# A graph attention layer: two of each batch's row gathers become 256 loads of one row each, from SP and ACT

## The chip, the cores and the metric

The kernel runs on one core of a Trainium2 chip. A core has five engines that run side by side: PE (TensorE, matrix products), DVE (VectorE), ACT (ScalarE), POOL (GpSimd) and SP (SyncE, which here only issues DMAs). Each works through its own instructions in order and waits for others by semaphores. DMAs are carried out by 16 DMA engines; they are issued by SP and ACT (hardware queues) and by POOL (a software queue). The metric is the time of one execution on the device in microseconds (us), as a median of several runs.

## The reference, cut to what matters

There are 12,500 nodes with 128 features and 412,500 edges, sorted by their target node; every edge has 64 features of its own. The layer normalizes the nodes, projects them, scores each edge from its two ends and its features, takes a softmax over the edges of each target, and adds the weighted sum of the source rows.

```
h = relu(layernorm(x)) @ W_node.T            # 4 heads of 32
e = edge_attr @ W_edge.T
att = leaky_relu(sum(concat[h[src], h[tgt], e] * a))
ex = exp(att - max over the edges of tgt)
w = ex / (sum of ex over the edges of tgt + (edges - degree) * exp(-m))
out = x + sum over the edges of tgt of w * h[src]
```

## The kernel before, in words

**Prologue** (lines 191 to 487). The nodes are normalized and projected once, and the results are written to a table in DRAM with one row of 144 floats (576 bytes, ROW) per node: for each head 32 values, two columns of ones, and the source's part of the score; at the end the target's part of the score for the four heads. Constants such as `least_b` (the byte address in the table of the lowest target of each chunk) and `pens` (where a segment begins) are made here too.

**Main loop** (lines 835 to 873). The edges are cut into chunks of 896 (7 tiles of 128, T = 7), 8 chunks make a batch (CB = 8), and there are 58 batches (NBT). A batch has 56 tiles; for each edge of a tile, one on each of the 128 partitions, the source's row is needed in `hs` (128 partitions x 56 tiles x 144 floats). There are two such buffers, one for the even and one for the odd batches. Tile 2 of each batch (FIRST) is not loaded from the table: its rows are projected anew by `normalize`, `project` and `keep_rows`. The other 55 are gathered by POOL in `gather` (line 547), one indirect DMA for each tile.

One turn `b` of the loop issues its work in this order, each engine taking its own part of it:

- SP: the indices of batch b+2 (line 187), then in `load` for batch b+1 the edge features `eft` (line 518), the targets `mem` (line 521), a register load of eight addresses (line 523), eight small loads `twb` from the table at register addresses (line 528), and `drawn` (line 533).
- POOL: `gather` for batch b+1. Ahead of its first gather stands a copy of `sums` into `gate` (line 550); `sums` is written by ACT at the end of the scatter of batch b-1 (line 684), the last user of the same `hs` buffer. So POOL begins only when that buffer is free.
- `weigh` of batch b (line 625): DVE waits until the rows have landed (`landed`, line 582; a wait on a semaphore that counts these loads), turns the scores (`zst`, line 629), then DVE and ACT in turn add them and make the leaky ReLU (lines 637 to 639, ACT's part L638), DVE makes two scans for the maximum of each segment (lines 641 and 643), ACT the exponentials (line 647), DVE the rest.
- SP: `pen` of batch b+1 (line 591), and the stores of finished outputs (line 820).
- `scatter` of batch b (line 655): DVE multiplies the rows by their weights (line 666); PE sums them with matrix products against `hot` (line 674) in three groups of chunks; ACT copies each group's results from PSUM to `r` (line 697), and `sums` in the last group (line 684).
- `normalize`, `begin` and `project` for batch b+1: ACT's L561, PE's products of edge features and targets (lines 602 and 606), DVE's masks (lines 597 to 621), among them `hot`, which waits until PE has used the old one.
- Every second batch `merge` (line 699), in which ACT makes two exponentials (lines 717 and 719) between two parts of DVE's work; then `keep_rows`; in about every fourth batch `finish` (line 784), where ACT makes an exponential (line 795) and 16 copies (line 810) that wait for DVE.

Everything is in this order because the loop stands under a manual schedule: no instruction is moved past another on its engine. Loads that go through `by_itself` (line 575) are counted by a semaphore of their own, and only `landed` waits for them.

Of the kernel before, what the change touches and what calls it, by code (L numbers as in the profile page):

```python
# [18 lines left out]
P = 128  # L19
# [11 lines left out]
SB = 4  # L31
# [26 lines left out]
LOGIT = EROW * 4  # L58
FIRST = 2
EPS = 1e-5  # L60


def tiles_of(sc):

    return [T if c < NCH - 1 else LAST for c in (2 * sc, 2 * sc + 1) if c < NCH]


# [37 lines left out]
def kernel(  # L105
# [4 lines left out]
    ahead: bass.AP,  # L110
    dstc: bass.AP,
    ef: bass.AP,
    w_node: bass.AP,
# [66 lines left out]
    row_sems = [tc.alloc_semaphore(f"rows{k}") for k in range(ROWSEMS)]  # L180
    row_done = [0] * ROWSEMS

    indices = ctx.enter_context(tc.tile_pool(name="indices", bufs=3))
# [7 lines left out]
    with (  # L191
# [7 lines left out]
        wn = p1.tile([P, D], F32, name="wn")  # L199
        nc.scalar.dma_start(wn, w_node)  # L200
        we = p1.tile([P, 2, K], F32, name="we")
        for s in range(2):
# [231 lines left out]
        for s in range(2):  # L434
            for j in range(SB):
                at = (2 * j + s) * H
                nc.vector.tensor_copy(wa3[s * K:(s + 1) * K, j, at:at + H], pe[s * K:(s + 1) * K, :])

        for g in range(NG):
            extent(g)  # L440
            load_extents(g + 2, min(g + 3, NG))
# [72 lines left out]
    def load(s):  # L514
# [17 lines left out]
        s.drawn = work.tile([P, D], F32, name="drawn")  # L532
        nc.sync.dma_start(s.drawn, drawn[:, s.b, :])
        s.hs = (work if s.b % 2 else even).tile([P, SB * CT, ROW], F32, name="hs")
        s.tiles = []
        for t in range(T):
            for sc in range(s.b * SB, (s.b + 1) * SB):
                held = tiles_of(sc) + [0, 0]
                for c in range(2):
                    i = (sc - s.b * SB) * CT + c * T + t  # L540
                    if t < held[c]:
                        if i != FIRST:
                            s.tiles.append(i)
                    else:
                        nc.vector.memset(s.hs[:, i, :], 0.0)
# [29 lines left out]
    def by_itself(load, group, sems, done, k):  # L575

        load.then_inc(sems[k], 16)
        done[k] += 16
        tc.add_to_no_dep_group(group, load.ins)
        tc.no_tile_sem_insts.add(load.ins.name)  # L580

    def landed(engine, group, sems, done, k, *what):
# [41 lines left out]

    def weigh(s):

        landed(nc.vector, f"rows{s.b}", row_sems, row_done, s.b % ROWSEMS, s.hs[:, :, :], s.ends[:, :, :, :])
        zst = work.tile([P, T, R], F32, name="zst")
# [4 lines left out]
        def grouped(what, g):  # L633
            return what.rearrange("r (t g i) -> r g t i", g=NQT, i=R)[:, g, :, :]

        for g in range(NQT):
            nc.vector.tensor_tensor(grouped(s.z, g), grouped(s.z, g), zst[g * R:(g + 1) * R, :, :], op=OP.add)  # L637
            nc.scalar.activation(grouped(att, g), grouped(s.z, g), AF.Identity, scale=0.2)  # L638
        nc.vector.tensor_tensor(s.z, s.z, att, op=OP.max)
        up = ps.tile([P, BANKS * 512], F32, name="up")[:R, :CE]  # L640
# [5 lines left out]
        for g in range(NQT):  # L646
            nc.scalar.activation(both[g * R:(g + 1) * R, 0, :, :], grouped(att, g), AF.Exp)  # L647
        for g in range(NQT):
            nc.vector.scalar_tensor_tensor(both[g * R:(g + 1) * R, 1, :, :], grouped(s.pen[:, 1:], g), -1.0 / BIG,  # L649
                                           grouped(m, g), op0=OP.mult, op1=OP.mult)  # L650
# [185 lines left out]
    with tc.manual_schedule():  # L836
        for b in range(-1, NBT):
            if b == -1:
                for k in range(2):
                    batch(k).ends = early[k]  # L840
                load_pen(batch(0))
            elif b + 2 < NBT:
                batch(b + 2).ends = index(b + 2)
            if b + 1 < NBT:
                load(batch(b + 1))
                gather(batch(b + 1), sums if b >= 1 else None)
            if b >= 0:
                s = batch(b)
                weigh(s)
                if b + 1 < NBT:  # L850
                    load_pen(batch(b + 1))
                for store in stores:
                    store()
                stores.clear()
                scatter(s)
            if b + 1 < NBT:
                normalize(batch(b + 1))
                begin(batch(b + 1))
                project(batch(b + 1))
            if b >= 0:  # L860
                first, last = merge_of(b)
                if b == last:
                    merge(first * CB, chunks_of(first, last))
                del batches[b]
            if b + 1 < NBT:
                keep_rows(batch(b + 1))
            if b == 3:
                count_windows()
            for b0, n, behind in parts():
                if behind == b:  # L870
                    stores.append(finish(work, ps, "up", em_ps, b0, n, b + 2 < NBT))
        for store in stores:
            store()
# [253 lines left out]
```

## Time and profile before

| | us |
|---|---|
| median of 3 runs | 4961.14 (4951.02 to 4962.55) |
| profiled execution | 4916.85 |
| its span | 4914.7 |
| busy: POOL | 3063.8 (62%) |
| busy: DVE | 1848.6 (38%) |
| busy: PE | 1798.9 (37%) |
| busy: ACT | 750.8 (15%) |

The profile is of one execution. Busy time counts work on data; instructions that load registers, wait, or issue DMAs from SP and ACT are not in it, so SP has no busy time at all though it issues hundreds of DMAs. Its instructions are seen in the timeline and in the view of one source line, with the letter q behind the engine's name. A line of the timeline gives start, duration, engine, line, operation, output<-input, the number of merged instructions, and in brackets the idle time before it with what ended it ("issue": nothing that the profile shows; "remote": an unknown releaser). A line of a group gives the count, the busy time in us and the mean of one in ns, then the idle time of the engine just before such instructions and what ended most of it.

### The profile page before, as it was taken

What the parts mean: (1) busy time and instruction counts of PE and PEld (TensorE: products, weight loads), DVE (VectorE), ACT (ScalarE), POOL (GpSimd) and SP (SyncE); (2) the same over time, 40 slices, a digit from 0 to 9 for tenths busy, and PEclk for the clock granted to TensorE, in tenths of its full rate; (3) what the DMA queues carried; (4) which work ended last, traced back from release to release, by engine and by line L of the source; (5) the groups of instructions that cost most, each with busy time, mean ns of one, the idle gap of its engine ahead of it and who ended that gap; (6) DMA issues with size and microseconds to landing.
All of it is one profiled execution on the core that took longest, in us unless ns stands there. A gap on an engine that the chain in (4) does not pass through costs nothing.

```text
span 4914.7 us, 22169 instructions
## 1 busy us (share of the span) xinstructions
PE 1798.9 (37%) x4479; PEld 719.8 (15%) x4479; DVE 1848.6 (38%) x3602; ACT 750.8 (15%) x2842; POOL 3063.8 (62%) x3295
## 2 busy tenths in 40 slices
PE   3133333343334333344334432433333333443243
PEld 2111111111111111111111111111111111111112
DVE  3424343424343343334342434334333433342335
ACT  3111111111111111111111111111111111111111
POOL 4446656666666666666666666666666666666661
PEclk7566666666666666667667665666666666666676
DMA  4333333333333333333332333333333333332431
GB/s 143 116 85 86 80 104 83 97 92 90 91 93 93 85 99 77 103 78 106 76 103 77 106 87 96 89 90 96 83 98 82 100 80 101 77 106 72 106 81 39
DMA packets 214923, 447.92 MB, mean 91 GB/s; under 512 B 86498, under 2 KB 119774, under 8 KB 214526
## 3 DMA queue, kind: packets, MB, share of 16 engines
q0 software_dynamic: 103136, 237.36, 21.1%
q1 hardware_dynamic: 108926, 201.71, 12.7%
q10 hardware_dynamic: 2720, 7.39, 0.4%
q14 instruction: 103, 0.84, 0.1%
q8 instruction: 38, 0.62, 0.1%
HBM read 427.11 MB, written 19.09 MB: 91 GB/s over the span
## 4 chain that ended last, share of the span: by engine, by line
another core or an unknown queue 33%; issue 25%; PE 16%; DVE 12%; ACT 11%; DVEq 1%; DMA 1%; ACTq 0%; SPq 0%
PE pa L674 8%; ACT r L697 7%; PE z L602 6%; PE z L606 2%; DVE up L641 2%; DVE m L643 1%; ACT both L647 1%; DVE z L637 1%; ACT a L638 1%; DVE acc L744 1%; ACT up L810 1%; DVE a L644 1%; DVE hs L666 1%; DVE a L735 1%
## 5 line engine op out<-in xcount | busy, mean ns | idle before, releaser
L552 POOL DMA_INDIRECT hs<-table,ends x3165 | 2997.2, 947 | 1072.4 <-issue 996.3
L674 PE MATMUL pa<-hs,hot 128*96 128x420 f32 (+2 forms) x2526 | 1037.1, 581 | 1872.7 <-issue 1244.7
L674 PEld LDWEIGHTS pa<-hs,hot 128*96 128x96 f32 (+2 forms) x2526 | 472.6, 192 | 2420.8 <-issue 2271.0
L697 ACT COPY r<-pa 32x35 f32<-32x35 f32 x1842 | 384.9, 209 | 2184.8 <-remote 1529.1
L621 DVE TENSOR_TENSOR hot<-exr,key 128x448 f32<-128x448 f32 x231 | 137.2, 621 | 1375.5 <-remote 1177.3
L666 DVE TENSOR_TENSOR hs<-hs,exr 128x924 f32<-128x924 f32 x461 | 476.8, 1101 | 0.0
L602 PE MATMUL z<-eft,wa 128*32 128x384 f32 (+1 forms) x928 | 470.5, 672 | 0.0
L563 PE MATMUL here<-ident,m 128*128 128x128 f32 x58 | 27.2, 469 | 1098.8 <-ACT m L561 995.0
L550 POOL COPY gate<-sums 32x1 f32<-32x1 f32 x56 | 9.9, 177 | 659.9 <-ACT sums L684 659.9
L638 ACT ACTIVATE a<-z 32x224 f32<-32x224 f32 x232 | 80.5, 347 | 958.3 <-DVE z L637 482.7
L606 PE MATMUL z<-mem,twb 128*32 128x512 f32 x464 | 183.9, 539 | 0.0
L563 PEld LDWEIGHTS here<-ident,m 128*128 128x128 f32 x58 | 10.4, 180 | 1128.2 <-ACT m L561 1024.2
L602 PEld LDWEIGHTS z<-eft,wa 128*32 128x32 f32 x928 | 116.0, 131 | 326.9 <-issue 326.7
L647 ACT ACTIVATE both<-a 32x224 f32<-32x224 f32 x232 | 89.9, 388 | 386.3 <-issue 207.8
L572 DVE COPY hs<-here 128x144 f32<-128x144 f32 x58 | 17.6, 304 | 347.7 <-PE here L568 183.4
L637 DVE TENSOR_TENSOR z<-z,zst 32x224 f32<-32x224 f32 x232 | 89.8, 387 | 134.2 <-issue 82.2
L597 DVE TENSOR_TENSOR mem<-mem,exr 128x896 f32<-128x896 int32 x116 | 120.2, 1074 | 30.3 <-issue 30.3
L744 DVE TENSOR_TENSOR acc<-acc,a 128x70 f32 x461 | 107.8, 234 | 33.5 <-issue 17.7
L641 DVE TENSOR_TENSOR_SCAN up<-pen,z 32x896 f32<-32x896 f32 x58 | 117.0, 2017 | 2.0
L643 DVE TENSOR_TENSOR_SCAN m<-pen,up 32x896 f32<-32x896 f32 x58 | 116.4, 2007 | 2.0
L649 DVE SCALAR_TENSOR_TENSOR both<-pen,m 32x224 f32<-32x224 f32 x232 | 88.2, 380 | 46.3 <-issue 44.5
L810 ACT COPY up<-a 32x224 f32<-32x224 f32 x208 | 70.7, 340 | 117.4 <-issue 59.9
(159 smaller groups left out, 1070.0 us busy)
## 6 DMA issues: line engine op xcount, KB each, us to landing
eft<-in_ef SPq DMA_DIRECT2D x58, 1792.0 KB
mem<-in_dstc SPq DMA_DIRECT2D x58, 896.0 KB
hs<-table,ends POOLq DMA_INDIRECT x3165
twb<-table SPq DMA_DIRECT2D x464, 0.5 KB
pen<-pens SPq DMA_DIRECT2D x58, 112.1 KB
table<-rows ACTq DMA_DIRECT2D x9, 648.0 KB
xg<-in_x SPq DMA_DIRECT2D x13, 448.0 KB
out<-xg SPq DMA_DIRECT2D x13, 448.0 KB
```

Of the source, the lines that this page charges most:

```text
L552: by_itself(nc.gpsimd.indirect_dma_start(out=s.hs[:, i, :], out_offset=None, in_=table[:, :], in_offset=bass.IndirectOffsetOnAxis(ap=s.end ...
L602: nc.tensor.matmul(s.z[:, part], wa3[:, j, :], s.eft[:, j, part], start=(j == 0), stop=False)
L606: nc.tensor.matmul(s.z[:, part], twb[:, s.b % 2, k, :], s.mem[:, k, part], start=False, stop=(k == 1))
L621: nc.vector.tensor_tensor(hot[:, :, q0:q0 + 2, :].rearrange("p t q r -> p q t r"), rows_ps[:, None, None, :].to_broadcast([P, 2, T, W]), k ...
L637: nc.vector.tensor_tensor(grouped(s.z, g), grouped(s.z, g), zst[g * R:(g + 1) * R, :, :], op=OP.add)
L641: nc.vector.tensor_tensor_scan(up, s.pen[:, :CE], s.z, 0.0, op0=OP.add, op1=OP.max)
L643: nc.vector.tensor_tensor_scan(m[:, ::-1], s.pen[:, CE:0:-1], up[:, ::-1], 0.0, op0=OP.add, op1=OP.max)
L647: nc.scalar.activation(both[g * R:(g + 1) * R, 0, :, :], grouped(att, g), AF.Exp)
L666: nc.vector.tensor_tensor(rows, rows, ex_ps[:, :n, q * H:(q + 1) * H, None].to_broadcast([P, n, H, HB]), op=OP.mult)
L674: nc.tensor.matmul(pa[:v * W, :v * H * AW], hot[:, i, q0:q0 + v, :].rearrange("p q r -> p (q r)"), by_chunk[:, q0:q0 + v, i, :], start=(i ...
L697: nc.scalar.copy(to, pa[q * W:(q + 1) * W, k:k + AW])
L744: nc.vector.tensor_tensor(cols, cols, put[:, i0 + i, :, :], op=OP.add)
```

## The change

Tiles 0 and 1 of every batch but the first are no longer gathered. Their 256 rows are loaded by 256 DMAs of one row each. The indices of these two tiles are loaded once into `at_sb`, one batch on each partition, and multiplied by the size of a row. `row_by_row` loads up to 32 of them into registers of an engine and then issues one DMA for each register. SP issues rows 0 to 79 after the other loads of the batch and rows 80 to 143 after `pen`. ACT issues the rest: 24 rows behind `normalize` of the batch before, 60 at the end of that turn, behind `merge` and `finish`, 16 between the two ACT stages of the weighing of the batch before, and 12 behind its exponentials. DVE waits for these loads by a semaphore of their own ahead of the wait for the gathers. The `hs` tile is now named a turn earlier (`open_rows`), since ACT's first rows are issued a turn earlier.

```diff
+RL = 32
+RT = 2
+SPROWS = (80, 144)
+ACTROWS = (168, 228, 244, RT * P)
...
+def by_row(b):
+
+    return RT if b >= 1 else 0
...
+    at_sb = const.tile([NBT, RT * P], I32, name="at_sb")
...
+        nc.scalar.dma_start(at_sb.rearrange("b (i p) -> b i p", i=RT),
+                            srcr.rearrange("(b i) p -> b i p", i=SB * CT)[:, :RT, :])
...
+        nc.vector.tensor_scalar(at_sb, at_sb, float(WIDE), None, op0=OP.mult)
...
+    def open_rows(s):
+
         s.hs = (work if s.b % 2 else even).tile([P, SB * CT, ROW], F32, name="hs")
...
-                        if i != FIRST:
+                        if i != FIRST and i >= by_row(s.b):
                             s.tiles.append(i)
...
+    def row_by_row(s, engine, kind, first, last):
+
+        if not by_row(s.b):
+            return
+        for r0 in range(first, last, RL):
+            n = min(RL, last - r0)
+            _, at = nc.values_load_multi_w_load_instructions(
+                at_sb[s.b:s.b + 1, r0:r0 + n], engines=[kind], min_val=0, max_val=(NB * P - 1) * WIDE,
+                skip_runtime_bounds_check_because="a src is below N, and N at most NB * P")
+            for r, v in enumerate(at, r0):
+                by_itself(engine.dma_start(s.hs[r % P:r % P + 1, r // P, :].bitcast(U8),
+                                           table_b[ds(v, WIDE)].rearrange("(o c) -> o c", o=1)),
+                          f"lone{s.b}", lone_sems, lone_done, s.b % ROWSEMS)
+
+    def rows_by_sp(s, k):
+
+        row_by_row(s, nc.sync, ENG.SP, (0, *SPROWS)[k], SPROWS[k])
+
+    def rows_by_act(s, k):
+
+        row_by_row(s, nc.scalar, ENG.Activation, (SPROWS[-1], *ACTROWS)[k], ACTROWS[k])
...
-    def weigh(s):
-
+    def weigh(s, ahead):
+
+        if by_row(s.b):
+            landed(nc.vector, f"lone{s.b}", lone_sems, lone_done, s.b % ROWSEMS, s.hs[:, :RT, :])
         landed(nc.vector, f"rows{s.b}", row_sems, row_done, s.b % ROWSEMS, s.hs[:, :, :], s.ends[:, :, :, :])
...
             nc.scalar.activation(grouped(att, g), grouped(s.z, g), AF.Identity, scale=0.2)
+        if ahead:
+            rows_by_act(ahead, 2)
...
             nc.scalar.activation(both[g * R:(g + 1) * R, 0, :, :], grouped(att, g), AF.Exp)
+        if ahead:
+            rows_by_act(ahead, 3)
...
                 load(batch(b + 1))
                 gather(batch(b + 1), sums if b >= 1 else None)
+                rows_by_sp(batch(b + 1), 0)
             if b >= 0:
                 s = batch(b)
-                weigh(s)
+                weigh(s, batch(b + 1) if b + 1 < NBT else None)
                 if b + 1 < NBT:
                     load_pen(batch(b + 1))
+                    rows_by_sp(batch(b + 1), 1)
...
             if b + 1 < NBT:
                 normalize(batch(b + 1))
+            if b + 2 < NBT:
+                open_rows(batch(b + 2))
+                rows_by_act(batch(b + 2), 0)
+            if b + 1 < NBT:
                 begin(batch(b + 1))
...
                     stores.append(finish(work, ps, "up", em_ps, b0, n, b + 2 < NBT))
+            if b + 2 < NBT:
+                rows_by_act(batch(b + 2), 1)
```

More of the change, by code (lines that the diff above doesn't have):

```diff
@@ L111 @@
     dstc: bass.AP,
+    srcr: bass.AP,
     ef: bass.AP,
@@ L181 @@
     row_done = [0] * ROWSEMS
+    lone_sems = [tc.alloc_semaphore(f"lone{k}") for k in range(ROWSEMS)]
+    lone_done = [0] * ROWSEMS
+    at_sb = const.tile([NBT, RT * P], I32, name="at_sb")
     indices = ctx.enter_context(tc.tile_pool(name="indices", bufs=3))
@@ L840 @@
                     batch(k).ends = early[k]
+                open_rows(batch(0))
                 load_pen(batch(0))
@@ L1112 @@
         "dstc": d.reshape(NC2, CE),
+        "srcr": s,
         "ef": np.ascontiguousarray(f).reshape(NSC, P, CE),
```

## The prediction

> **What bounds the kernel now.** I read the busy times and the costliest groups of the page first, then the timelines of POOL, ACT, PE and SP around 2300 to 2620 us, where four batches repeat with a mean of 80.2 us (the four `sums` copies after 2368.53 come at 2449.64, 2528.94, 2609.91 and 2689.3; (2689.3 - 2368.5)/4). The two groups of the page:
>
> ```profile
> L552 POOL DMA_INDIRECT hs<-table,ends x3165 | 2997.2, 947 | 1072.4 <-issue 996.3
> L550 POOL COPY gate<-sums 32x1 f32<-32x1 f32 x56 | 9.9, 177 | 659.9 <-ACT sums L684 659.9
> ```
>
> POOL issues 55 gathers a batch and then stands still until ACT has written `sums`, the last act of a scatter: 660 us in 56 waits, 11.8 each. The timeline of POOL shows one turn: the last gather of a batch, the wait, the next batch.
>
> ```profile
> 2435.97 0.94 POOL L552 DMA_INDIRECT hs<-table,ends  x1 [0.31 <-issue]
> 2437.22 0.94 POOL L552 DMA_INDIRECT hs<-table,ends  x1 [0.30 <-issue]
> 2449.85 0.18 POOL L550 COPY gate<-sums 32x1 f32<-32x1 f32 x1 [11.69 <-ACT sums L684]
> 2450.66 0.98 POOL L552 DMA_INDIRECT hs<-table,ends  x1 [0.63 <-DVE hot L621]
> ```
>
> A gather comes every 1.25 us (2437.22 - 2435.97), so 55 take 68.75. What ends last in a scatter is odd: PE's records of the third group end at 2501.6, yet ACT gets the second group at 2526.28 (timelines of PE and ACT):
>
> ```profile
> 2496.77 4.87 PE L674 MATMUL pa<-hs,hot 128*64 128x280 f32 x14 [3.67 <-issue]
> 2526.28 2.64 ACT L697 COPY r<-pa 32x35 f32<-32x35 f32 x12 [29.57 <-remote]
> ```
>
> In all batches that I looked at, this release comes 7 to 9 us behind the end of the gather that runs beside it (2519.1 and 2526.3; 2438.2 and 2446.9; 2598.4 and 2607.2), and `sums` 2.7 us later. I take it as it stands: PE's results come free when POOL's gathers end. So the loop is 68.75 of gathers, some 10.5 to `sums`, 1 to the next gather: 80.2. POOL's loop bounds the kernel; the chain of DVE, PE and ACT is shorter by what it waits there.
>
> **What goes.** Two gathers of 1.25 us: 2.5 us a batch off the loop, 77.7 instead of 80.2. In 56 turns that is 140 us, if nothing else becomes late.
>
> **What comes.** 256 DMAs of one row (576 bytes) a batch, 144 from SP, 112 from ACT. The nearest row is the `twb` load of SP, also at a register address. In the first batch, where nothing holds SP back (instructions of line 528, then the register load of line 523, durations in ns, min/median/max):
>
> ```profile
> L528 SPq MOVE twb<-table x8: 29/29/38, 235.9 to 239.7; - x8
> L528 SPq DMA_DIRECT2D twb<-table x8: 321/356/413, 236.0 to 239.8; - x8
> L523 SPq TENSOR_LOAD <-least_b x58: 700/1048/1073, 234.8 to 4791.3; - x58
> ```
>
> A MOVE and a DMA instruction with the gaps between them come about every 0.47 us. One row may be cheaper than the 32 pieces of a `twb`, but `eft` with 512 pieces is issued in 0.44 us and `drawn` with 128 in 0.41, so the number of pieces hardly counts. The bounds of a row: 0.40 (0.36 and a gap, no MOVE) below; above, 2.1, the pace in later batches while `eft` and `mem` are in flight (timeline of SP, first batch and a later one):
>
> ```profile
> 235.99 4.09 SPq L528 DMA_DIRECT2D twb<-table  x8
> 2464.81 16.62 SPq L528 DMA_DIRECT2D twb<-table  x8
> ```
>
> I take 0.47, since the row loads stand behind these eight and `pen` and `out`, issued at 2420.40 and 2421.21 beside a running gather, took 0.75 and 0.40 again. A load of 32 registers is not shown; 8 take 1.05 on SP, so 1.05 to 4.2; I take 1.5, nearer to one fixed cost, as DVE needs 0.6 for 8. There are five such loads on SP, five on ACT (one each for the 24, 16 and 12 rows, two for the 60).
>
> **SP.** 144 x 0.47 = 67.7, loads 5 x 1.5 = 7.5. Its own work from `eft` to `ends` takes 8.2 in the first batch (232.80 to 241.0), 10.8 with the 2.6 that `mem` waits for PE, and 29 at the slow pace (2460.0 to 2489.1); I take 20. Sum 95 us a batch, where it has 80: SP's present rest (2260.9 us of waiting for PE in 50 waits, 45 each, in the table of waits) is 30 short of the 75 that come. In its queue `pen` now stands behind 80 rows, `out` and the next `ends`, `eft` and `mem` behind all 144. Most have time; rows that land late hold the next weighing directly, by the wait added ahead of `zst` on DVE, behind which the whole batch is queued.
>
> **ACT.** Its rows lie on the chain from `sums` to the next weighing. Now, `sums` to the first `a` of L638: 15.6 to 15.7 us in a plain batch (2449.64 to 2465.24, 2609.91 to 2625.59), 27.8 with a merge, 39.4 with a merge and a finish:
>
> ```profile
> 2370.36 0.49 ACT L561 ACTIVATE m<-drawn,drawn_shift,drawn_rstd 128x128 f32<-128x128 f32 x1
> 2372.69 0.61 ACT L717 ACTIVATE up<-dif 128x528 f32<-128x528 f32 x1 [1.83 <-DVE dif L715]
> 2399.77 5.92 ACT L810 COPY up<-a 32x224 f32<-32x224 f32 x16 [8.58 <-DVE a L802]
> 2407.90 0.35 ACT L638 ACTIVATE a<-z 32x224 f32<-32x224 f32 x1 [2.21 <-issue]
> ```
>
> The 24 rows behind L561 take 24 x 0.47 + 1.5 = 12.8; of that 1.8 lie in the idle time before L717, 11 delay the merge, and what DVE does for merge and finish. The 60 rows behind the finish take 28.2 + 3 = 31.2, in front of `a`, with the 2.2 shown there as cover. So `sums` to `a` becomes: plain 2.3 + 12.8 + 31.2 = 46.3; merge alone about 47; merge and finish 39.4 + 11 + 31.2 = 81.6, less 2. The 16 rows between `a` and L647 take 9 where ACT now idles 7 (7.02 before 2417.99): 2 more. The 12 behind them (7.1) lie in ACT's wait for the first results of PE, 18 to 23 us. From `a` to `sums` it is 32.7 in the first batch, where no gather holds the results, and 41.7 in the tightest later one (2407.90 to 2449.64); I take 36. Four batches: 2 x (46.3 + 38) + (47 + 38) + (79.6 + 38) = 371, 93 each.
>
> **The rest.** One DMA for `at_sb` and its multiplication in the prologue: under 2 us (a like load on ACT's queue takes 0.42), beside the x loads. The memsets move for the last batch alone. 84 rows of ACT before the first weighing (40 us) lie beside gather 0. The bytes are the same, now by hardware queues, which took 12.7% of the DMA engines' span. The second wait on DVE costs its issue, about 0.05, if the rows are there.
>
> **Sum.** SP 95, ACT's chain 93, POOL's loop 77.7: the slowest gives 95 a batch, 14.8 more, x 56 = 829 us. The profiled execution took 4916.85 (span 4914.7, 2.15 around it) and would take 5746; the median of the runs shown is 4961.14, 44 above it (4951.02 to 4962.55), which I add: 5790.
>
> By the low ends (row 0.40, load 0.6, `a` to `sums` 32.7) SP needs 72, and ACT's plain batches (2.3 + 33.6 + 1.8 + 32.7 = 70) fall under POOL's 77.7; but the finish batch has 39.4 + 8.4 + 25.2 + 32.7 = 106, so a mean of 84.8 and 258 us more: 5220. By the high ends of the load (4.2) and SP's own 29, SP needs 118: 7080. The likeliest case's own range is 5220 to 6700.
>
> **Rivals.** (1) Faster: the rows hide. The one place that decides is the finish batch on ACT: 84 rows and 3 loads lie in series there, the four batches gain 4 x 2.5 = 10 us, and in the weighing behind a finish ACT waits 3.1 us for the second results (before 2446.88); they win as long as 84 rows and the loads stay under 13, a row under 0.15. Then POOL's loop alone counts: 4961 - 140 = 4821. For it: POOL is the bound and ACT is idle for 85% of the span; against it: no DMA instruction with a register address took under 0.32 undisturbed. [...] (2) In between: a row of 0.2 to 0.33, where only the finish batches lose, or other batches' gains pay for them: 4950 to 5220. (3) SP's slow pace lasts as long as row loads and gathers are both in flight: 144 x 2.1 = 302 a batch, far over 10,000 us; with it for a third of the rows, 95 + 48 x 1.6 = 172, some 10,000. The mid-batch `pen` and `out` at normal pace speak against it. (4) It does not do what it says: rows land after the gathers and the wait moves to the new semaphore. That is the forecast's SP case.
>
> **Numbers.** Forecast (5220 to 6700) 0.66; faster 0.15; in between 0.10, of which 0.02 within 0.3%; SP slow or loads at their high end (over 6700) 0.09. A change of 0.3%, 15 us, is about what the runs can tell from none. Faster 0.15, same 0.02, slower 0.83. For 8 in 10 I take in the faster case and cut the top: 4810 to 6700.
>
> **What would show it.** POOL's issues 53 a batch at 1.25 us, and its wait for `sums` longer than 11.8; SP nearly without waiting for PE at `eft`; on ACT gaps of 12 and 30 us before L717 and L638; DVE waiting ahead of `zst` for rows. A pair of MOVE and DMA well under 0.3 us would make the forecast wrong, and so would a finish batch no longer than before.

## The result and the profile after

| | before | changed |
|---|---|---|
| median of 4 runs, us | 4959.84 (4951.02 to 4962.55) | 7437.84 (7432.59 to 7440.15) |
| span of the profiled execution, us | 4914.7 | 7436.9 |
| mean from one `sums` to the next (55 of them), us | 80.6 | 125.3 |

The ratio is 1.4999 (95% interval 1.4973 to 1.5025). It was forecast slower, at 5790 us; it came out slower by far more, above the top of the range, 6700. One thing must be known to read what follows: beside this result and beside the first ten experiments the kernel before took 4917 to 4960 us (called "slowed" here), while in the last three groups of runs the same kernel took 4109 to 4117 us (called "free"). Every ratio below is to the runs of its own group; the difference between the two kinds is taken up at the end of the experiments.

The spans differ by 2522 us. From the first `sums` to the last, 55 batches, lie 4430.9 us before and 6892.3 after, so 2461 of it is in the batches, 44.8 each; 23 stand ahead of the first `sums`, which comes at 368.8 and not at 346.1, and 38 behind the last.

The page of the changed kernel: the chain that ended last, by engine and by line (line 611 is the row load in `row_by_row`, 607 its register load), and three groups, where gate is now line 569 and the gather 571.

```profile
issue 34%; ACTq 27%; SPq 20%; PE 8%; DVE 6%; ACT 3%; DMA 1%; another core or an unknown queue 1%; DVEq 0%
...
L571 POOL DMA_INDIRECT hs<-table,ends x3051 | 2885.3, 946 | 1039.6 <-issue 935.4
...
L681 ACT ACTIVATE a<-z 32x224 f32<-32x224 f32 x232 | 80.3, 346 | 3930.9 <-issue 2622.6
...
L569 POOL COPY gate<-sums 32x1 f32<-32x1 f32 x56 | 9.9, 177 | 3285.9 <-ACT sums L731 3285.9
```

POOL issues 53 gathers a batch, each as long as before (946 ns), and no longer bounds the kernel: it waits 3286 us for `sums`, 58.7 in each of 56 waits, where it waited 11.8. ACT's first leaky ReLU of a weighing (`a`) waits for "issue", that is for ACT's own row loads. The timeline of ACT, one turn:

```profile
3615.41 0.15 ACT L731 COPY sums<-pa 32x1 f32<-32x1 f32 x1 [0.86 <-PE pa L721]
...
3618.28 90.74 ACTq L611 DMA_DIRECT2D hs<-table  x84
3709.14 0.35 ACT L681 ACTIVATE a<-z 32x224 f32<-32x224 f32 x1 [91.40 <-issue]
...
3740.56 0.15 ACT L731 COPY sums<-pa 32x1 f32<-32x1 f32 x1 [0.86 <-PE pa L721]
```

ACT's 84 rows (24 and 60) stand between `sums` and the next `a` and take 91 us; from `a` to the next `sums` are 31.4. POOL's gathers start with the same `sums` (3616.43 to 3682.33), so the rows and the gathers run together, and the weighing and the scatter after both. Before, weighing and scatter lay beside the gathers. The timeline of SP, the 64 rows in two loads behind `pen`, and the 80 rows in three loads of the next turn, most of which find no gather running:

```profile
3624.45 80.06 SPq L611 DMA_DIRECT2D hs<-table  x64
...
3714.32 39.50 SPq L611 DMA_DIRECT2D hs<-table  x80
```

A row costs SP 1.25 us in the one stretch and 0.49 in the other, on average. Counted from the trace in steps of 5 us (starts of row loads and of gathers):

```
from      SP  ACT  POOL        from      SP  ACT  POOL
3595      15   12     0        3660       2    2     4
3620       3    7     4        3680       1    1     2
3630       2    2     4        3690       7   12     0
3640       2    1     4        3695      16    8     0
```

Without a gather 13 to 16 rows go out in 5 us (0.33 us each); within one, two on SP and two on ACT (2.5 us each), and the slow pace lasts until some 8 us behind the last gather. The view of line 611 (durations in ns, min/median/max) shows that it is not the DMA instruction alone: the MOVE ahead of it, 29 ns as a rule, takes up to 1.4 and 1.7 us too.

```profile
L611 SPq MOVE hs<-table x8208: 2/29/1407, 316.9 to 7388.7; - x196
L611 SPq DMA_DIRECT2D hs<-table x8208: 2/228/1408, 317.0 to 7388.7; - x196
L611 ACTq MOVE hs<-table x6384: 2/29/1667, 264.9 to 7339.8; - x200
L611 ACTq DMA_DIRECT2D hs<-table x6384: 2/235/1667, 265.0 to 7339.9; - x200
```

### The profile page after: what moved, and what is told of

Its sections match the earlier page's. It is cut to its first block, busy times and chain, and to the rows that moved or that the text cites. A ratio compares the mean times of both kernels' runs of the same rounds, so it can differ in the third digit from the quotient of the medians.

```text
span 7436.9 us, 51872 instructions
## 1 busy us (share of the span) xinstructions
PE 1611.4 (22%) x4479; PEld 657.2 (9%) x4479; DVE 1849.1 (25%) x3603; ACT 750.5 (10%) x2842; POOL 2951.9 (40%) x3181
## 3 DMA queue, kind: packets, MB, share of 16 engines
q0 software_dynamic: 99488, 228.94, 11.6%
## 4 chain that ended last, share of the span: by engine, by line
issue 34%; ACTq 27%; SPq 20%; PE 8%; DVE 6%; ACT 3%; DMA 1%; another core or an unknown queue 1%; DVEq 0%
ACTq L611 25%; SPq L611 17%; PE pa L721 8%; SPq L607 2%; ACTq L607 2%; DVE hs L713 2%; ACT a L681 1%; DVE z L680 1%; ACT r L744 1%; DMA xg<-in_x 0%; SPq L545 0%; DVE acc L791 0%; ACT up L857 0%; ACT both L692 0%
## 5 line engine op out<-in xcount | busy, mean ns | idle before, releaser
L571 POOL DMA_INDIRECT hs<-table,ends x3051 | 2885.3, 946 | 1039.6 <-issue 935.4
L721 PE MATMUL pa<-hs,hot 128*96 128x420 f32 (+2 forms) x2526 | 907.1, 523 | 5401.8 <-DVE hs L713 5401.8
L721 PEld LDWEIGHTS pa<-hs,hot 128*96 128x96 f32 (+2 forms) x2526 | 421.2, 171 | 5872.4 <-issue 5725.2
L672 DVE STREAM_TRANSPOSE zst<-hs 128x224 f32<-128x224 f32 x58 | 33.4, 577 | 1796.9 <-DVEq L625 1771.2
L643 PE MATMUL z<-eft,wa 128*32 128x384 f32 (+1 forms) x928 | 419.5, 611 | 0.0
L864 DVE TENSOR_TENSOR xg<-up,xg 128x448 f32<-128x448 f32 (+2 forms) x30 | 16.4, 589 | 403.7 <-DMA xg<-in_x 391.6
L764 ACT ACTIVATE up<-dif 128x528 f32<-128x528 f32 (+2 forms) x30 | 17.9, 596 | 955.4 <-issue 952.4
```

Of the source, the lines that this page charges most:

```text
L571: by_itself(nc.gpsimd.indirect_dma_start(out=s.hs[:, i, :], out_offset=None, in_=table[:, :], in_offset=bass.IndirectOffsetOnAxis(ap=s.end ...
L643: nc.tensor.matmul(s.z[:, part], wa3[:, j, :], s.eft[:, j, part], start=(j == 0), stop=False)
L721: nc.tensor.matmul(pa[:v * W, :v * H * AW], hot[:, i, q0:q0 + v, :].rearrange("p q r -> p (q r)"), by_chunk[:, q0:q0 + v, i, :], start=(i ...
```

## The experiments

**Theory A:** while POOL issues its gathers, the instructions of SP and ACT are held up, to some 0.7 to 1.4 us each, so a row (a MOVE and a DMA) has two prices, 0.33 and 2.5; ACT's rows in front of `a` then last until the gathers have ended. **Rival B:** the row loads of SP and of ACT get in each other's way, and either engine alone would go at 0.33. The prediction's single price, 0.47, is the third.

### The gain alone, and one engine alone

The 256 row loads become one plain load by SP of as many rows:

```diff
     def rows_by_sp(s, k):
-        row_by_row(s, nc.sync, ENG.SP, (0, *SPROWS)[k], SPROWS[k])
+        if k == 0 and by_row(s.b):
+            by_itself(nc.sync.dma_start(s.hs[:, :RT, :], table[:RT * P, :].rearrange("(p t) c -> p t c", t=RT)),
+                      f"lone{s.b}", lone_sems, lone_done, s.b % ROWSEMS)
     def rows_by_act(s, k):
-        row_by_row(s, nc.scalar, ENG.Activation, (SPROWS[-1], *ACTROWS)[k], ACTROWS[k])
+        return
```

> All 256 single-row loads are replaced by one plain load of 256 neighbouring rows of the table on SP, so tiles 0 and 1 hold rows of the wrong nodes; POOL gathers 53 tiles as in the changed kernel. This is the gain side alone. If POOL's loop bounds the kernel before and what follows the gathers keeps its length, 2.5 us a batch go: about 4820 us. Rival: what PE's results wait for has nothing to do with the end of the gathers, and the chain from one scatter to the next keeps its 80.2 us: 4960.

Measured: 4813.52 us, ratio 0.9715 (0.9699 to 0.9731). POOL's wait for `sums` is 704 us in 56 waits, about as before. Two gathers less are worth 137 us beside the runs of its group (4950.26): the part of the prediction on what goes was right.

Then one engine's rows alone become plain loads; the other keeps its own one by one.

```diff
     def rows_by_act(s, k):
-        row_by_row(s, nc.scalar, ENG.Activation, (SPROWS[-1], *ACTROWS)[k], ACTROWS[k])
+        if k == 0 and by_row(s.b):
+            r0 = SPROWS[-1] - P
+            by_itself(nc.scalar.dma_start(s.hs[r0:, 1, :], table[:P - r0, :]),
+                      f"lone{s.b}", lone_sems, lone_done, s.b % ROWSEMS)
```

> SP's 144 row loads stay; ACT's 112 rows are replaced by one plain load on ACT's queue (rows of the wrong nodes). Theory A, shared pace: while POOL issues gathers, and some 8 us behind, the instructions of SP and ACT go one per 0.70 us together, whatever they are; then a row of SP alone costs 1.4 us there and 0.33 outside, and a batch needs 115 to 120 us: 6700 to 7000 us. Theory B, the two hardware queues slow each other: SP alone issues a row in 0.33 throughout, 144 take 48 us, the batch stays at POOL's 78: about 4850. The prediction's constant price of 0.47: 5200 at most.

Measured: 7286.84 us, ratio 1.4712 (1.4681 to 1.4743). Timeline of SP, the 80 rows and the 64 behind `pen`:

```profile
3641.28 36.89 SPq L611 DMA_DIRECT2D hs<-table  x80
...
3681.55 74.03 SPq L611 DMA_DIRECT2D hs<-table  x64
```

With no row loads on ACT, SP has the same two paces: beside the gathers again two rows in 5 us. The time lies above the 6700 to 7000 that was expected, and the reason is plain: there SP and ACT shared one slow pace, so that SP alone would pay 1.4 us a row, but a row costs each of them 2.5, alone or not. The other way round, with SP's 144 rows in two plain loads (the same edit in `rows_by_sp`):

> ACT's 112 row loads stay; SP's 144 rows are replaced by two plain loads on SP's queue (rows of the wrong nodes). Theory A: the 84 rows between sums and the next weighing cost 1.4 us each until the gathers have ended, some 53 of them, the rest 0.33, so 88 us to the first a of the weighing and 120 a batch: 6900 to 7200 us. Theory B: 0.33 each throughout, 34 us in plain batches, 72 in those with a finish: 85 a batch, about 5200.

Measured: 7213.41 us, ratio 1.4563 (1.4534 to 1.4593), at the top of what A gave; ACT's 84 rows take 87.25 us in the plain batch at 3772. B falls: either engine alone costs nearly all of it. In the run with SP alone, DVE's additions in `merge` (line 794) take 232 ns while SP is slow and 232 ns otherwise, so not every engine is held in the same way.

### Which part of POOL's work does it

POOL's gathers become one plain load a batch, but for the last batch (this and the next two kernels keep all 256 row loads):

```diff
-        for i in s.tiles:
+        spans = [(0, FIRST), (FIRST + 1, SB * CT)] if not by_row(s.b) else [(FIRST + 1, SB * CT)]
+        for a, e in spans if s.b < NBT - 1 else []:
+            by_itself(nc.gpsimd.dma_start(s.hs[:, a:e, :], table[:(e - a) * P, :].rearrange("(p t) c -> p t c", t=e - a)),
+                      f"rows{s.b}", row_sems, row_done, s.b % ROWSEMS)
+        for i in s.tiles if s.b == NBT - 1 else []:
```

> All row loads of SP and ACT stay as in the changed kernel; POOL's 53 gathers of a batch are replaced by one plain load of 6784 neighbouring rows (rows of the wrong nodes, but for the last batch), so POOL issues one DMA a batch. Theory A: the rows cost 0.33 throughout, and ACT's chain gives 65 to 70 us in plain batches and 105 with a finish: 4500 to 4900 us. Theory B, or rows that slow each other by their number: the rows keep their 1 us and more, 6500 us and above.

Measured: 4499.41 us, ratio 0.9084 (0.9066 to 0.9102). To this, 53 copies a batch on POOL in the place of the gathers (`for i in s.tiles: nc.gpsimd.tensor_copy(idle[:, 1, :], idle[:, 0, :])`, 408 ns each):

> As the run without gathers (rows from SP and ACT, one plain load of POOL for all other tiles), but POOL also makes 53 copies of 128x256 values a batch that nobody reads. Theory A in the form that the gathers' descriptors slow SP and ACT: rows stay at 0.33 us, about 4500 us as without the copies. The form that any work of POOL slows them: 1.4 to 2.8 us a row and 6500 us and more.

Measured: 4527.65 us, ratio 0.9122 (0.9096 to 0.9149). And the 53 gathers as 53 plain loads by POOL, with the same bytes:

```diff
-            by_itself(nc.gpsimd.indirect_dma_start(
-                out=s.hs[:, i, :], out_offset=None, in_=table[:, :],
-                in_offset=bass.IndirectOffsetOnAxis(ap=s.ends[:, i // CT, 0, i % CT:i % CT + 1], axis=0)),
+            by_itself(nc.gpsimd.dma_start(s.hs[:, i, :], table[i * P:(i + 1) * P, :]),
```

> The changed kernel with plain loads from POOL in place of the indirect gathers, one for each of the 53 tiles (rows of the wrong nodes). If what slows SP and ACT is that POOL writes the descriptors of many DMAs, it is as slow as the changed kernel as long as POOL issues for 60 us and more a batch: 6800 to 7500 us. If it is the indirect form (the reading of indices) alone: rows at 0.33 us and about 4500.

Measured: 4429.96 us, ratio 0.8925 (0.8900 to 0.8951). Its page and the view of its row loads (line 609):

```profile
L571 POOL DMA_DIRECT2D hs<-table x3051 | 1605.2, 535 | 144.9 <-issue 78.7
```

```profile
L609 SPq MOVE hs<-table x8208: 29/29/38, 242.2 to 4378.0; - x196
L609 SPq DMA_DIRECT2D hs<-table x8208: 224/228/2232, 242.3 to 4378.0; - x196
```

No MOVE is longer than 38 ns. The queue of POOL moved the same number of packets as with the gathers (99,488), and faster. So neither POOL's being busy nor its packets slow SP and ACT; of the forms tried, only the indirect one does. The limit of this run: the plain loads are issued within some 29 us of a batch, the gathers in 66.

### Any instruction, and from when

To the kernel before, waits on SP behind `pen` that are met already when they come (24 instructions a batch in the trace):

```diff
+                    for _ in range(48):
+                        nc.sync.wait_ge(twb_sems[b % 2], s.twb_count)
```

> The kernel before, with 24 instructions more on SP behind each load of pen: waits on a count that was reached long ago, which touch no DMA, no memory and no data. They stand in SP's idle time while POOL gathers. Theory A (any instruction of SP is slow while gathers run, 0.7 to 1.4 us each): 17 to 34 us for the 24, against 0.05 each elsewhere; the time of the kernel stays at 4960 as long as SP keeps some rest. Theory D (only DMA instructions are held up, by the queues): the 24 pass in 1 to 2 us.

Measured: 4977.62 us, ratio 1.0038 (1.0027 to 1.0050).

```profile
L854 SPq EVENT_SEMAPHORE  x1368: 3/700/1423, 324.4 to 4898.2; - x196
```

In this run an instruction of SP that moves nothing and waits for nothing takes 0.7 us at the median and 1.4 at most. The 24 of one batch took 23 us (2450.7 to 2473.7): the first three came 0.06 to 0.08 us apart, the next sixteen mostly 1.4, and the last five, 9 us behind the last gather (2464.48), came in a row again. So theory D, named with this run, falls: the slowing is one of SP's instructions, not of DMAs alone. Half of the rows (`RT = 1`, `SPROWS = (40, 72)`, `ACTROWS = (84, 114, 122, RT * P)`: 72 rows on SP, 56 on ACT, one gather less than before):

> The change with one tile instead of two: 72 rows by SP, 56 by ACT, POOL gathers 54. Theory A: ACT's 42 rows between sums and the next weighing still last until the gathers have ended, 84 us to the weighing instead of 94, 116 us a batch: about 6900 us. If rows cost what they cost by their number alone, half of the loss goes: about 6200 us. The prediction's price of 0.47 us a row: 5000 to 5300 us.

Measured: 6167.63 us, ratio 1.2426 (1.2390 to 1.2463), below the 6900 that A gave and above the prediction's price. It is what the second case gave, rows that cost by their number alone (6200), so the time by itself speaks against A; the timeline of ACT tells the two apart:

```profile
3036.97 0.15 ACT L731 COPY sums<-pa 32x1 f32<-32x1 f32 x1 [0.86 <-PE pa L721]
...
3039.10 62.65 ACTq L611 DMA_DIRECT2D hs<-table  x41
3103.20 0.35 ACT L681 ACTIVATE a<-z 32x224 f32<-32x224 f32 x1 [63.90 <-issue]
```

ACT's first 21 rows beside these gathers go out at 9 in 5 us, a register load among them, the others at 2 in 5 us: still two paces, not one price by number. But the slow pace is not there from the first gather on, as A has it: here it sets in 11 us behind it (3048.8 and 3038.0), and on SP in the run with SP alone 5 us behind it (3671.1 and 3666.1). With its end 8 us behind the last gather, it looks like something that fills while gathers come and drains afterwards. That gives theory C: the rate of the gathers counts, not their being there.

### A slower pace of gathers

To the changed kernel, three copies on POOL behind each gather (`for _ in range(3): nc.gpsimd.tensor_copy(idle[:, 1, :], idle[:, 0, :])`):

> The changed kernel with three copies on POOL (about 0.41 us each, as measured in the run with a busy POOL) behind every gather, so that a gather comes every 2.6 us or so and not every 1.25; nothing is left out. 53 gathers then take about 138 us a batch. Theory C (something that the gathers fill at their rate and that drains meanwhile, full after some 10 us): at half the rate it never fills, rows come at 0.33 us all the time, ACT has its 84 rows done 35 us behind sums, and POOL alone sets the loop: 138 and 2 to 10 us, about 145 a batch, 8300 to 8900 us; POOL waits little for sums. Rival D (any gather in progress slows the others, whatever the rate): a row stays at 2.5 us and more for the whole 138 us, ACT's rows last until 8 us behind the last gather, and 31 us of weighing and scatter follow: about 185 a batch, 10,300 to 11,200 us, with POOL waiting 45 us a batch. In between: rows at about 1.3 us, the middle of the two, at which 84 rows of ACT take 110 us, still under POOL's 138, so the time would be C's, and the rows' pace in the trace tells it.

Measured: 7792.91 us, ratio 1.5848 (1.5824 to 1.5872); a gather every 2.46 us. Timeline of ACT (line 615 is the row load here), the plain turn:

```profile
3767.13 0.15 ACT L735 COPY sums<-pa 32x1 f32<-32x1 f32 x1 [0.86 <-POOL idle L578]
...
3770.00 33.40 ACTq L615 DMA_DIRECT2D hs<-table  x84
3866.98 0.35 ACT L685 ACTIVATE a<-z 32x224 f32<-32x224 f32 x1 [97.52 <-DVE z L684]
```

84 rows take 33.4 us and not 91, in the midst of gathers, and `a` then waits for DVE, which waits for the gathers. That the time is long is POOL's own 130 us a batch (53 x 2.46), and not the 138 expected, since three copies take 1.33 us together and the gap ahead of a gather is mostly 0.15 (3628.18 to 3628.33), where it was 0.30; so the time lies below C's 8300 to 8900 and far below D's. D falls, and of C this much holds: at half the rate the slowing is nearly gone (no MOVE of ACT takes longer than 30 ns, none of SP longer than 548), though the gathers run nearly all the time. That something fills and drains is not shown, and the copies also stand between the gathers, so the pace is not parted from that.

The gain alone had shown that a gather less pays where nothing takes its place on SP and ACT. So the kernel before, with a second tile of the first 22 batches projected anew like tile 2:

```diff
+NX = 22
+SECOND = 1
...
+        s.own = (FIRST, SECOND)[:1 + (s.b < NX)]
...
-                        if i != FIRST:
+                        if i not in s.own:
...
-        nc.vector.tensor_scalar(s.hT, turned_ps, 0.0, None, op0=OP.max)
-        nc.tensor.matmul(row_ps, s.hT, wall, start=True, stop=True)
+        for k in range(len(s.own)):
+            nc.vector.tensor_scalar(s.hT[k], turned_ps[k], 0.0, None, op0=OP.max)
+        for k in range(len(s.own)):
+            nc.tensor.matmul(row_ps[k], s.hT[k], wall, start=True, stop=True)
```

> The kernel before, with tile 1 of the first 22 batches projected anew like tile 2 (no row loads by SP or ACT at all), so POOL issues 54 gathers in those batches; nothing is left out. Theory: POOL's loop is the bound and a gather is worth 1.25 us where nothing else comes late (the block load gave 147 us for 112 gathers, 1.3 each), so 22 x 1.25 = 27 us less, ratio 0.9945, 4932. Against it: 22 more gathers in the prologue (27 us of POOL there, if POOL bounds it) and a longer normalize and keep_rows on ACT and DVE (two instructions of 0.5 and 0.3 us each, in the 10 us to sums): then 4960 or up to 4975.

Measured: 4947.37 us, ratio 1.0061 (1.0048 to 1.0075). The first `sums` comes at 376.2 and not 346.1: 30 us for 22 more gathers in the prologue, the whole loss. The 22 batches gain nothing, 81.1 each against 81.0 (376.2 to 2159.8, and 346.1 to 2128.7): `sums` now comes 12.6 us behind the last gather there on average, where it came 11.4 behind (from the gather's end), which eats up the 1.25 us of the gather that is gone. It is no better version.

### Where the pace turns, and a second kind of runs

Four kernels were to show where between 1.25 and 2.46 us the slowing ends, and whether a slower pace would let PE's results come in time in the kernel before. The edit is one copy behind each gather, of the columns named.

The changed kernel with 256 columns (a gather every 1.55 us), and with 8 (every 1.34):

> The changed kernel with one copy of 0.41 us on POOL behind each gather: a gather every 1.57 us (0.98 + 0.44 + 0.15), 83 us a batch; nothing is left out. If 1.57 is slow enough for rows at 0.36: SP and ACT set the loop as the prediction had it, 85 to 95 us a batch, 5300 to 5900 us. If it is not: rows at 2.5 us until 8 us behind the gathers, sums to a about 110, and 31 to the next sums: 140 a batch, 8200 to 8400. Rows that begin fast and slow down later in a batch would give something between, 100 to 120 a batch, 6100 to 7200.

> The changed kernel with one copy of 8 columns on POOL behind each gather, some 0.1 to 0.2 us: a gather every 1.3 to 1.45 us. If the rate decides sharply at 1.25, rows at 0.36 and 5300 to 5900 us. If 1.3 is still too fast: as the changed kernel or a little longer by the longer gathers, 7400 to 8000.

The kernel before with 8 columns (every 1.34 us), and with 128 (every 1.45):

> The kernel before with one copy of 8 columns on POOL behind each gather: 55 gathers at 1.3 to 1.45 us, 72 to 80 us a batch, in place of 68.75; nothing is left out. If the late release of PE's results is the same slowing and ends at this pace, sums comes before the last gather and the loop is the gathers alone plus 1: 73 to 81 a batch, ratio 0.92 to 1.01. If the release has another cause and stays 10 to 12 us behind the last gather: 84 to 92 a batch, ratio 1.04 to 1.13.

> The same with a copy of 128 columns, some 0.25 us: a gather every 1.41 us or so, 78 us a batch. With prompt results 79 a batch, ratio about 0.985; with results 10 to 12 us behind the last gather 89 a batch, ratio about 1.11. Partly slowed: the lag shrinks with the pace, ratio near 1.03.

Measured, in this order: 4938.83 us, ratio 1.2018 (1.1999 to 1.2036); 4357.57, ratio 1.0608 (1.0592 to 1.0624); 4439.28, ratio 1.0802 (1.0788 to 1.0817); 4777.06, ratio 1.1622 (1.1606 to 1.1638). All ratios are to 4109.49, the kernel before in this group: here nothing was slowed to begin with, so these four say nothing of where the pace turns. In the two with row loads the median from one row to the next is 0.32 us; `sums` comes in time in all four (POOL waits for it 14 us in sum at most), so POOL's paced gathers set the loop (55 x 1.34 = 73.8 a batch with 8 columns in the kernel before). The next group asked what the change itself does on such runs:

> The changed kernel once more, unchanged. Beside a kernel before of 4916 to 4960 us: 7440, ratio 1.50. Beside one of about 4110 (no slowing by gathers): rows at 0.36 us, ACT's chain as in the run with the 8-column copy (84 rows 33 us, sums to sums 66 to 86, the finish batch the longest), SP 144 rows in 54 us and some 20 of its own; POOL's gathers 53 x 1.2 = 64 hidden: about 4300, ratio 1.04 to 1.06.

> The kernel before with a copy of 8 columns behind each gather, a gather every 1.34 us, 73.8 us a batch. Beside a kernel before of 4916 to 4960 us: if 1.34 is slow enough for prompt results, 4440 as measured on the other chip, ratio 0.90; if not, 10 to 12 us of lag on top, 84 to 86 a batch, 5030 to 5130, ratio 1.02 to 1.04. Beside one of about 4110: 4440 again, ratio 1.08.

Measured: the changed kernel 4355.81 us (4342.80 to 4360.12) beside 4116.69, **ratio 1.0585 (1.0567 to 1.0603)**; the kernel before with the small copy 4451.64, ratio 1.0814 (1.0796 to 1.0832). Its ACT, a plain turn and one with merge and finish:

```profile
2253.69 0.15 ACT L731 COPY sums<-pa 32x1 f32<-32x1 f32 x1 [0.85 <-PE pa L721]
...
2256.55 33.27 ACTq L611 DMA_DIRECT2D hs<-table  x84
2289.95 0.35 ACT L681 ACTIVATE a<-z 32x224 f32<-32x224 f32 x1 [33.94 <-issue]
...
2321.43 0.15 ACT L731 COPY sums<-pa 32x1 f32<-32x1 f32 x1 [0.86 <-PE pa L721]
...
2324.27 8.50 ACTq L611 DMA_DIRECT2D hs<-table  x24
2332.82 0.61 ACT L764 ACTIVATE up<-dif 128x528 f32<-128x528 f32 x1 [9.07 <-issue]
...
2354.04 22.45 ACTq L611 DMA_DIRECT2D hs<-table  x60
2376.62 0.35 ACT L681 ACTIVATE a<-z 32x224 f32<-32x224 f32 x1 [24.58 <-issue]
...
2407.66 0.15 ACT L731 COPY sums<-pa 32x1 f32<-32x1 f32 x1 [0.86 <-PE pa L721]
```

and POOL, the gate copies at the ends of these two turns:

```profile
2321.64 0.18 POOL L569 COPY gate<-sums 32x1 f32<-32x1 f32 x1 [0.68 <-ACT sums L731]
...
2407.87 0.18 POOL L569 COPY gate<-sums 32x1 f32<-32x1 f32 x1 [18.82 <-ACT sums L731]
```

The gathers come every 1.25 us, as in the slowed runs, and rows go out at full pace beside them. A plain turn is 67.7 us, as POOL's gathers need it (53 x 1.25 + 1.2); the turn with the finish 86.2, in which POOL waits 18.8. The last group gives the trace of the kernel before on a free run:

> The kernel before once more, unchanged. On a chip of the 4110 kind: sums comes no later than the last gather of a batch and not 11 to 12 us behind it, a batch is 55 gathers of 1.2 us and 1 (66 to 67 us), POOL's wait for sums near 0, ACT's r copies released by PE at once. On one of the 4950 kind: as its first profile.

> The kernel before with the 8-column copy behind each gather, once more. On a chip of the 4950 kind: 4440, ratio 0.90, if a gather every 1.34 us is slow enough for prompt results; 5030 to 5130, ratio 1.02 to 1.04, if not. On one of the 4110 kind 4440 to 4455 again, ratio 1.08.

Measured: 4109.72 us, ratio 1.0002 (0.9991 to 1.0014), and 4438.97, ratio 1.0793 (1.0762 to 1.0825). The views of lines 552 and 550 and the timeline of SP in the kernel before, free; the same eight `twb` loads of its slowed profile, 16.62 us, stand in the prediction:

```profile
L552 POOL DMA_INDIRECT hs<-table,ends x3165: 943/947/1924, 81.4 to 4052.1; - x198
...
L550 POOL COPY gate<-sums x56: 193/198/205, 220.8 to 4015.4; 32x1 f32<-32x1 f32 x56
...
2479.03 3.61 SPq L528 DMA_DIRECT2D twb<-table  x8
```

Gathers of the same length; but the gate copy never waits, a batch is 68.8 us (55 x 1.25, and the copy lies in a gap), `sums` is written 36 us ahead of its gate copy (2324.72 and 2360.35), and eight `twb` loads take 3.6 us and not 16.6. So the 11 us of waiting in each batch of the kernel before, the late results of PE and SP's slow `twb` go together, and all three are missing in the free runs; that they have one cause is inferred from that. 645 us of the 797 between the two spans are in the 55 batches (4430.9 less 3786.1), 149 ahead of the first `sums` (346.1 and 197.2).

What makes a run slowed stays open. The same program does both with the same work; it is not the execution within a group, where all runs agree; the records give the number 3 for the chip both in the group beside 4950 us and in the one beside 4117, so the number doesn't tell them apart. All slowed groups came before all free ones, so something may have changed in between; the records don't say what. Each run here was recorded, so none can say whether the recording has a part in it. The number of instructions in the traces speaks rather against that: in the slow stretch of the changed kernel (3632 to 3682) they have 2.3 instructions per us, of all engines together, just behind it (3692 to 3740) 10.9, and beside the gathers of the free run (2260 to 2320) 11.7. Not shown either: where between 1.25 and 2.46 us the pace turns on slowed runs.

## Why the prediction was wrong, point by point

**What goes: right.** 140 us were forecast for two gathers a batch, 137 measured with the block load (slowed).

**What bounds the kernel: right, with a cause unseen.** "PE's results come free when POOL's gathers end" was taken as it stands. The free run shows that it was a sign: in the slowed runs instructions elsewhere were being held up while gathers came. I read what is most likely a symptom of the very effect that decided the case and asked no more of it.

**The price of a row: the step that failed.** "I take 0.47, since ... `pen` and `out`, issued at 2420.40 and 2421.21 beside a running gather, took 0.75 and 0.40 again." On the slowed runs a row has two prices, 0.33 us without gathers, below my low bound of 0.40, and 2.5 with them, above my high bound of 2.1. The two witnesses were too few instructions: on SP the first three waits of 24 were fast too, and ACT's first 21 rows. The sign that mattered was at hand. The prediction shows line 528 in the first batch alone; over the whole run of the kernel before, the same view reads:

```profile
L528 SPq MOVE twb<-table x464: 5/696/1397, 235.9 to 4807.8; - x155
L528 SPq DMA_DIRECT2D twb<-table x464: 3/698/1683, 236.0 to 4809.2; - x155
```

A MOVE, 29 ns in the first batch, takes 0.7 us at the median. So the slow pace was the rule and the first batch the exception. The high bound stood in the right row, but with the wrong condition: "the pace in later batches while `eft` and `mem` are in flight". The free run has these in flight at the same place and takes 3.6 us. Nor did the range use that bound: its ends vary the register load and SP's own work, and a row only down to 0.40. ACT's 84 rows and their loads were to cost 44 us and took 91.4; from `sums` to `a` it was 93.7, and with 31.4 from `a` to `sums` the turn is 125.1, where the forecast had 84 for a plain one.

**The rival that named the mechanism.** Rival (3), a slow pace "as long as row loads and gathers are both in flight", had the mechanism, and was priced out of reach at 10,000 us: it let each of SP's 144 rows be slow. But rows slow only until 8 us behind the gathers, and the next gathers wait for `sums`, so the loop settles at gathers (66) + 8 + the rest of the rows + weighing and scatter, 125 us. A rival whose slowing and cause feed back on each other has to be followed through one turn.

**The chains on free runs.** There the mechanism of the forecast is the one that acts, and its sizes can be read. The changed kernel is 223.6 us longer in its span: 13 turns with a finish and an early one take 86.7 on average against 68.8 (250 us more), the 41 others 67.7 (46 less), and 22 stand ahead of the first `sums`, less 2 at the end. The prediction had named the finish batch as "the one place that decides".

| term, us | predicted | free | slowed |
|---|---|---|---|
| row without its register load | 0.47 | 0.33 | 0.33 and 2.5 |
| load of up to 32 registers (median SP, ACT) | 1.5 | 2.2, 1.7 | 2.0, 1.2 |
| ACT's 84 rows and 3 loads, plain turn | 44 | 33.9 | 91.4 |
| `sums` to `a`, plain | 46.3 | 36.3 | 93.7 |
| `sums` to `a`, merge and finish | 79.6 | 55.2 | 97.4 |
| `a` to `sums` | 38 | 31.5 | 31.4 |
| SP, a batch | 95 | 72 to 74 | with the turn |
| loop, mean | 95 | 72.5 | 125.3 |

The finish turn was mis-sized by 31 us, 117.6 against 86.2 to 86.7. About 18 of it is merge and finish themselves: without the row loads ahead of L764 and `a` (9.07 and 24.58) `sums` to `a` is 21.5, and not the 39.4 of before, which came from a slowed profile. Some 6.5 is the rows (33.7 and not 40.2, their cover taken off), and 6.5 the way from `a` to `sums`. SP's 72 to 74 is read from its timeline (rows behind `pen` start at 2254.24, 2328.01 and 2400.72); its waits of 1600 us for `eft` and 1680 for `pen` in the free kernel before are all but gone. So SP's queue and ACT's chain both come to about 72.5 a batch there, and no run parts them.

The free loss is a third of what I gave (0.058 against 5790 / 4961 - 1 = 0.167), and the slowed one is three times as much. The forecast lies between two kinds of runs, and is right for neither. That the low end of the range, 258 us more, is near the free loss of 239 is luck: both its plain turn (77.7 against 67.7) and its finish turn (106 against 86.2) are too long, as is the turn of before that they are compared with (80.2 against 68.8).

**The price in rival (1).** Free, 0.33 us a row is small beside the 3.8 us (median) from the issue of a `twb` load to its landing, and 84 of them in front of `a`, 33.3 us in the plain turn at 2256.55, still decide; slowed, a row beside the gathers is 2.5. The bound that rival (1) gives, a row under 0.15 us, leaves nothing for the three register loads; with them at 1.5 us it is 0.10. Either is well below the 0.33 measured.

## What to carry to other kernels

Price many small DMAs by the issuing engine's instructions, and by where they stand: here 84 rows in front of the instruction that releases the next stage cost 33.3 us free and 90.7 slowed, though ACT is idle for 85% of the span of the kernel before. Before a price is taken from a quiet place of the trace, look over the whole run for instructions of no work (a MOVE, a wait that is met) that take longer than in that place: here a MOVE of 29 ns in the first batch had a median of 696 over the run, something held the engine, and the price was that of a long row of such instructions, not of the first few. And if the same program has been seen at two times 20% apart (here 4960 and 4110 us), an effect that one of them lacks may be what the profile shows.

## What the runs showed of the hardware

- On slowed runs, beside POOL's indirect gathers at one every 1.25 us, instructions of SP and ACT take up to 1.7 us, a MOVE of 29 ns included, and each of the two engines gets through one about every 1.35 us (37 in 50 us), from 5 to 11 us behind the first gather to 8 us behind the last. With a gather every 2.46 us, and copies between them, 84 rows take 33.4 us and not 91; nor is it so with plain loads by POOL at 0.54 us each, or with its copies alone.
- On free runs the same gathers (947 ns, one every 1.25 us) do nothing of the kind (no MOVE of a row load takes longer than 38 ns), and a row load of 576 bytes at a register address goes out every 0.33 us on SP and ACT at the same time.
- A load of 12 to 32 registers has a median of 2.2 us on SP and 1.7 on ACT (free), one of 8 registers 1.05 on SP (kernel before, slowed).
